# Where the second layer's expert outputs are summed: an internal array, or the output itself

## The chip, the cores and the metric

The kernel runs on one core of a Trainium2 chip. The core has a matrix engine (PE), a vector engine (DVE), a scalar engine (ACT), a general engine (POOL), and a queue engine (SP) that mostly issues transfers. Each engine runs its own list of instructions in order, and the lists are tied together by semaphores. Transfers are carried by 16 DMA engines that all queues share. The metric is the device time of one execution in microseconds (us); the median of three runs before the change is 1024.19 us (1023.56 to 1030.92).

## The reference

Two transformer layers run over `x` of 4 sequences x 512 tokens x 256 features. Each layer is a cross-attention followed by a mixture of experts in which every token goes to its two best experts out of eight. Only the end of the second layer matters here:

```
x = x + L1_xattn(layernorm(x), ctx)           # residual after the attention
logits = layernorm(x) @ Wg                    # 8 experts, the best two of each token
comb   = softmax(top 2) * alpha               # weight of each (token, expert)
for e in range(8):
    a = gelu(hdn_e @ fc1_w[e] + fc1_b[e])     # 256 -> 1024
    y = a @ fc2_w[e] + fc2_b[e]               # 1024 -> 256
    out += y * comb[:, e]
return x + out
```

The result of a token is thus its residual (with the biases `fc2_b`, weighted) plus two weighted expert rows. 2048 tokens times two choices are 4096 rows. With the inputs of the reference the experts of the second layer get 748, 469, 588, 538, 499, 487, 330 and 437 rows.

## The kernel before

**Routing.** For each of the four sequences `route_steps(L1, b)` computes the two experts of each token, and scatters the normalised rows (256 features, the token's number, the weight) into the internal array `rows`, one region for each expert (L851, an indirect DMA on POOL). Then it adds the weighted biases to the residual `x[b]` in SBUF (L888) and stores `x[b]` as 512 KB into the internal array `acc` (L889, on the SP queue). `acc` has 2048 rows for the tokens, and 128 spare rows behind them, which are filled with zeros at the very start of the kernel (L129, a DMA on POOL).

**The expert tiles.** `moe(L1, ...)` then walks over tiles of 128 rows. Each expert's rows are cut into tiles, and the last tile of an expert is usually not full. For 748, 469, ... 437 rows that makes 6 + 4 + 5 + 5 + 4 + 4 + 3 + 4 = 35 tiles, 4480 places for 4096 rows; the very last tile has 437 - 3 x 128 = 53 rows. The program has code for up to 39 tiles: 35 unconditionally, the rest under `tc.If`, which these inputs don't enter. For each tile,

- `load_rows` (L989, SP) fetches 128 rows; `load_w` (L973, SP) fetches the expert's two weight matrices where the expert changes;
- `turn` transposes the rows on PE and scales them (L1011, L1017), and computes in `to` (L1004, DVE) where each row of the result belongs: the token's number, or, for a place that holds no row, a spare row (`aside`, L947: 2048 plus the partition's number);
- `up` multiplies by the first matrix (L1031) and applies gelu (L1040, ACT); `down` multiplies by the second (L1052), weights the rows on DVE (`yw`, L1056), and adds them to `acc` by an indirect DMA with addition, issued on POOL (L1069).

Since the additions all go into one array, each of these indirect DMAs waits until the one before has landed. The order of PE's work is written out by hand, as is SP's in the expert parts. On the other engines, and for SP in the second attention, a planner at build time places the instructions.

**The end.** After the last tile `layer1_experts` copies the 2048 token rows of `acc` into the kernel's output `out` (L1163), a DRAM to DRAM transfer of 2.1 MB on the SP queue. It waits for all additions. Then the program ends: SP waits for the semaphores of all transfers, and the engines drain and meet (all at L1238).

**In the first layer** the same function stores its rows differently (L1059): a plain indirect DMA into `ys`, whose bounds check has `oob_is_err=False`. There `aside` is a row number behind the array's end, so that places without a row are not written at all.

Of the kernel before, what the change touches and what calls it, by code (L numbers as in the profile page):

```python
# [8 lines left out]
F32 = mybir.dt.float32  # L9
# [4 lines left out]
ALU = mybir.AluOpType  # L14
# [3 lines left out]
P = 128  # L18
NB = 4
S = 512  # L20
# [3 lines left out]
D = 256  # L24
# [31 lines left out]
def two_layers(ctx: ExitStack, tc: tile.TileContext, io, out):  # L56
    nc = tc.nc
# [11 lines left out]
    dram = ctx.enter_context(tc.tile_pool(name="dram", bufs=1, space=bass.MemoryType.DRAM))  # L69
# [4 lines left out]
    def t4(shape, name, dt=F32):  # L74
        return k4.tile(shape, dt, tag="k4", name=name)
# [4 lines left out]
    def tsmall(shape, tag, dt=F32):  # L80
        return sm.tile(shape, dt, tag=tag, name=tag, bufs=2 if tag[:3] in ("rt_", "tp_", "tt_") else None)
# [7 lines left out]
    def mm_ps(name):  # L89
        return ps_m.tile([P, 512], F32, tag="m", name=name)  # L90
# [30 lines left out]
    nc.gpsimd.tensor_copy(tile_f, tile_i)  # L121

    rows = dram.tile([EX * REGION, ROW], F32, tag="rows", name="rows")
    acc = dram.tile([NB * S + P, D], F32, tag="acc", name="acc")

    ys = dram.tile([2 * NB * S, D], F32, tag="ys", name="ys")
    zeros = t4([P, ROW], "zeros")
    nc.gpsimd.memset(zeros, 0.0)
    nc.gpsimd.dma_start(out=acc[NB * S :, :], in_=zeros[:, 0:D])  # L129
    def after(a, b, why):  # L130
        info = mybir.DependencyInfo(mybir.DependencyClass.Sync, mybir.DependencyReason.DATA)
        tc.add_manual_dep(a.ins, b.ins.name, info, reason=why)
# [10 lines left out]
    x = []  # L143
# [42 lines left out]
    for e in range(EX):  # L186
        i = nc.gpsimd.dma_start(
            out=rows[e * REGION : (e + 1) * REGION, :].rearrange("(p k) r -> p k r", p=P),
            in_=zeros.unsqueeze(1).to_broadcast([P, REGION // P, ROW]),
# [5 lines left out]
        out=ys[:, :].rearrange("(p k) d -> p k d", p=P),  # L195
        in_=zeros[:, 0:D].unsqueeze(1).to_broadcast([P, 2 * NB * S // P, D]),
# [497 lines left out]
    def top2(lg, ne, pick):  # L694

        shape = [P, NT, ne]
        by_e = desc[:, ET0 - ne :].unsqueeze(1).to_broadcast(shape)

        def over(v):
            return v.unsqueeze(2).to_broadcast(shape)  # L700

        m = []
        l = lg
        for k in range(2):
            mk = tsmall([P, NT], f"tp_m{k}")
            nc.vector.tensor_reduce(mk, l, AX.X, ALU.max)
            o = pick[:, k]
            nc.vector.tensor_tensor(o, l, over(mk), ALU.is_equal)
            nc.vector.tensor_tensor(o, o, by_e, ALU.mult)
            at = tsmall([P, NT], f"tp_at{k}")  # L710
            nc.vector.tensor_reduce(at, o, AX.X, ALU.max)
            nc.vector.tensor_tensor(o, o, over(at), ALU.is_equal)
            m.append(mk)
            if k == 0:
                l = tsmall(shape, "tp_l")
                nc.vector.scalar_tensor_tensor(l, o, TAKEN, lg, ALU.mult, ALU.add)
        d = tsmall([P, NT], "tp_d")
        nc.vector.tensor_tensor(d, m[1], m[0], ALU.subtract)
        e = tsmall([P, NT], "tp_e")
        nc.scalar.activation(e, d, AF.Exp)  # L720
        den = tsmall([P, NT], "tp_den")
        nc.vector.tensor_scalar(den, e, 1.0, None, ALU.add)
        w = tsmall([P, 2, NT], "tp_w")
        nc.vector.reciprocal(w[:, 0], den)
        nc.vector.tensor_tensor(w[:, 1], e, w[:, 0], ALU.mult)
        return w
# [53 lines left out]
    def route_steps(L, b):  # L780
# [22 lines left out]
        st = L.state.pop(b)  # L803
# [3 lines left out]
        w = top2(lg, ne, pick)  # L807
# [11 lines left out]
        r = const.tile([P, NT + 1, ne], F32, tag=f"run{L.n}{b}", name=f"run{L.n}_{b}")  # L819
# [4 lines left out]
        at = tsmall([P, NT, ne], "rt_atp")  # L824
# [23 lines left out]
        for k in range(2):  # L848
            for t in range(NT):

                i = nc.gpsimd.indirect_dma_start(  # L851
                    out=rows[:, :],
                    out_offset=bass.IndirectOffsetOnAxis(ap=pos_i[:, k, t : t + 1], axis=0),
                    in_=buf[:, k, t, :], in_offset=None,
                    bounds_check=EX * REGION - 1, oob_is_err=False,
# [25 lines left out]
        for k in range(0, NT, 2):  # L881
# [4 lines left out]
                )  # L886
            xs = x[b][:, k : k + 2, :]
            nc.vector.tensor_tensor(xs, op.rearrange("p (j d) -> p j d", d=D), xs, ALU.add)  # L888
        nc.sync.dma_start(out=acc[b * S : (b + 1) * S, :].rearrange("(t p) d -> p t d", p=P), in_=x[b])  # L889
        yield  # L890

    def tile_table(L):
# [59 lines left out]
    def ring_slots(L):  # L952

        slots = []
        if L.n == 0:
            for s in range(RING):
                if s % 2 == 0:
                    t = tbig(f"w0s_{s}").rearrange("p (h w) n -> p h (w n)", w=2)
                h = 2 * (s % 2)
                slots.append((t[:, h, :], t[:, h + 1, :]))  # L960
        else:
            for s in range(RING):
                w1 = res.tile([P, W1ROW], F32, tag=f"ctxT{s}", name=f"w1s_{s}")
                w2 = t8([P, FF1 // P * D], f"w2s_{s}")
                slots.append((w1, w2))
        for s in range(RING):
            for part in range(2):
                ring_load(L, slots[s], part, slice(0, 1))
        return slots
# [5 lines left out]
    def moe(L, slots, side=iter(())):  # L975
# [69 lines left out]
        def down(i):  # L1045
            w2 = slots[i % RING][1]
            aT = aTs.pop(i)
            rt = rts.pop(i)
            to = tos.pop(i)
            op = mm_ps(f"y{n}_{i}")[:, 0:D]  # L1050
            for f in range(nf):
                nc.tensor.matmul(  # L1052
                    op, aT[:, f, :], w2[:, f * D : f * D + D], start=(f == 0), stop=(f == nf - 1)
                )
            y = t4([P, D], f"yw{n}_{i}")
            nc.vector.tensor_scalar(y, op, rt[:, D + 1 : D + 2], None, ALU.mult)  # L1056
            where = bass.IndirectOffsetOnAxis(ap=to[:, 0:1], axis=0)
            if n == 0:
                st = nc.gpsimd.indirect_dma_start(  # L1059
                    out=ys[:, :], out_offset=where, in_=y, in_offset=None,  # L1060
                    bounds_check=2 * NB * S - 1, oob_is_err=False,
                )
                if y_stores:
                    tc.declare_no_dep(st.ins, group="ys", reason="no two tiles have the same row")
                    after(st, ys_fill, "the rows are filled before")
                tc.add_to_no_dep_group("ys", st.ins)
                y_stores.append(st)
            else:
                nc.gpsimd.indirect_dma_start(  # L1069
                    out=acc[:, :], out_offset=where, in_=y, in_offset=None,  # L1070
                    bounds_check=NB * S + P - 1, oob_is_err=True, compute_op=ALU.add,
                )

        def run(lo, hi, at=None):
            for i in range(lo, min(lo + 2, hi)):
                load_rows(i)
            for i in range(lo, min(lo + RING, hi)):
                for part in range(2):
                    load_w(i, part)
            turn(lo)  # L1080
            for i in range(lo, hi + 1):
                if i < hi:
                    if i + 2 < hi:
                        load_rows(i + 2)
                    up(i)
                    if i + RING < hi:
                        load_w(i + RING, 0)
                    if i + 1 < hi:
                        turn(i + 1)
                if i > lo:  # L1090
                    down(i - 1)
                    if i - 1 + RING < hi:
                        load_w(i - 1 + RING, 1)
                if i >= 8:
                    next(side, None)
                if i == at:
                    used.append(
                        nc.values_load(
                            total[0:1, 0:1], engines=None, min_val=0, max_val=TILES,
                            skip_runtime_bounds_check_because="at most TILES: one tile of each expert is not full",  # L1100
                        )
                    )
# [57 lines left out]

    def layer1_experts():
        moe(L1, ring_slots(L1))
        nc.sync.dma_start(  # L1163
            out=out.rearrange("b s d -> (b s) d").rearrange("(q r) d -> q (r d)", q=16),
            in_=acc[0 : NB * S, :].rearrange("(q r) d -> q (r d)", q=16),
        )

    with tc.manual_schedule(engines={mybir.EngineType.PE}):
        route = layer0_attention()
        with tc.manual_schedule(engines={mybir.EngineType.SP}):  # L1170
            sts = layer0_experts(route)
        layer1_attention(sts)
        with tc.manual_schedule(engines={mybir.EngineType.SP}):
            layer1_experts()
# [67 lines left out]
```

## Time and profile before

| Quantity | us |
|---|---|
| median of three runs | 1024.19 |
| the profiled execution, as timed | 1006.65 |
| its span, first to last instruction | 1004.9 |
| first matmul of a second-layer tile | 732.30 |
| last matmul of a tile ends (982.53 + 7.07) | 989.60 |
| last weighting on DVE ends (989.64 + 0.48) | 990.12 |
| last addition issued on POOL | 991.39 |
| copy `out<-acc` issued on SP | 995.22 |

The span of the profile is the time from the first instruction to the last on the core. The profiled execution's own time is 1.75 us above its span, and the median of the runs without a profile is 17.5 us above that. Times in the views are counted from the start of the span. A line of the chain of waits gives start, length and the work (engine, tile, source line); "POOLq" or "SPq" is an engine's instruction queue, with its waits and issue, rather than its arithmetic.

### The profile page before, as it was taken

Reading aid. Unit: us, or ns where it says so; the run is one execution under the profiler, and the core shown is the slowest. Engines: PE = TensorE matmul, PEld = TensorE weight load, DVE = VectorE, ACT = ScalarE, POOL = GpSimd, SP = SyncE. Lnnn points to the kernel's source line nnn. Section 1 sums busy time; section 2 is a strip of 40 time slices with the busy share of each in tenths; the row PEclk is TensorE's granted clock in tenths of the full one; section 3 lists DMA queues with packets and bytes.
Section 4 is the critical chain, followed back from the end, with each engine's and each line's share of the span. In section 5 each row is a group of like instructions: output and inputs, shape, how many; then the busy total and the mean of one; then the engine's idle time right before and its main releaser. Section 6 shows DMA issues by size and latency. Waiting matters only on the chain.

```text
span 1004.9 us, 15208 instructions
## 1 busy us (share of the span) xinstructions
PE 906.9 (90%) x5506; PEld 674.1 (67%) x5506; DVE 441.4 (44%) x1257; ACT 328.4 (33%) x727; POOL 225.5 (22%) x263
## 2 busy tenths in 40 slices
PE   5888989988989999889989989999489999999993
PEld 2445464635579997456656656657289999999993
DVE  6555473725623322854755666656511111111110
ACT  2222221220111111565754555554132323232230
POOL 3310103031502222000120330422601221121211
PEclk9899999998999999989999999999589999999997
DMA  8999802011149794500000101101816868678963
GB/s 319 283 255 237 267 1 92 24 57 44 57 156 293 245 313 163 174 1 2 22 1 2 64 22 43 64 1 38 299 33 183 256 203 259 179 252 240 326 191 100
DMA packets 55033, 144.65 MB, mean 144 GB/s; under 512 B 6454, under 2 KB 32877, under 8 KB 48776
## 3 DMA queue, kind: packets, MB, share of 16 engines
q1 hardware_dynamic: 39224, 104.98, 31.2%
q0 software_dynamic: 15440, 38.63, 15.2%
q8 instruction: 46, 0.75, 0.3%
q14 instruction: 35, 0.29, 0.1%
q10 hardware_dynamic: 288, 0.00, 0.0%
HBM read 142.02 MB, written 42.14 MB: 183 GB/s over the span
## 4 chain that ended last, share of the span: by engine, by line
PE 45%; issue 4%; ACT 4%; DVE 4%; DMA 2%; POOL 1%; SPq 0%; POOLq 0%; ACTq 0%; DVEq 0%
PE hp L1031 12%; PE y L1052 11%; PE s L578 6%; PE a2t L601 5%; PE o L626 4%; DVE p L587 2%; ACT p L591 2%; PE q L562 1%; DMA acc<-yw,to 1%; PE v L480 1%; PE k L466 1%; PE wo L641 1%; POOL rowbuf L769 1%; PE ht L1011 1%; ACT L591 1%
## 5 line engine op out<-in xcount | busy, mean ns | idle before, releaser
L1031 PEld LDWEIGHTS hp<-hT,w1s 128*128 128x128 f32 x1120 | 133.3, 195 | 3.6 <-DVE hT L1017 1.9
L1031 PE MATMUL hp<-hT,w1s 128*128 128x128 f32 x1120 | 133.8, 279 | 1.2 <-DVE hT L1017 1.2
L1040 ACT ACTIVATE aT<-hp,w1s 128x128 f32<-128x128 f32 x280 | 76.2, 384 | 168.4 <-issue 168.4
L1052 PE MATMUL y<-w2s,aT 128*128 128x256 f32 x560 | 126.5, 379 | 0.0
L1052 PEld LDWEIGHTS y<-w2s,aT 128*128 128x128 f32 x560 | 103.8, 190 | 12.7
L1069 POOL DMA_INDIRECT acc<-yw,to x35 | 54.0, 1541 | 212.1 <-DVE to L1004 137.1
L587 DVE CUSTOM_DVE_ANT_0 p<-s,mbias 128x1024 f32<-128x1024 f32 x64 | 75.8, 1220 | 57.5 <-PE s L578 57.5
L591 ACT ACTIVATE p<-p,s_nm 128x1024 f32<-128x1024 f32 x64 | 73.4, 1147 | 68.1 <-DVE s_nm L587 68.1
L1056 DVE TENSOR_SCALAR yw<-y,row 128x256 f32<-128x256 f32 x63 | 30.5, 484 | 136.5 <-PE y L1052 136.5
L601 PEld LDWEIGHTS a2t<-ident,p 128*128 128x128 f32 x512 | 57.1, 143 | 46.7 <-issue 25.3
L601 PE MATMUL a2t<-ident,p 128*128 128x128 f32 x512 | 72.7, 283 | 12.0 <-ACT a2T L606 5.6
L851 POOL DMA_INDIRECT rows<-rowbuf,rt_posi x64 | 64.0, 1000 | 57.3 <-DVE rt_posi L831 20.9
L578 PE MATMUL s<-kT,q2T 64*128 64x512 f32 x256 | 72.1, 669 | 2.1 <-DVE s_nm L587 2.1
L1017 DVE TENSOR_SCALAR hT<-ht,w1s 128x128 f32<-128x128 f32 x70 | 25.5, 406 | 94.7 <-PE ht L1011 90.9
L626 PE MATMUL o<-a2T,v 128*64 128x128 f32 x1024 | 63.3, 276 | 1.7 <-ACT kT L471 1.1
L626 PEld LDWEIGHTS o<-a2T,v 128*64 128x64 f32 x1024 | 55.4, 137 | 11.5 <-issue 7.5
L606 ACT COPY a2T<-a2t 128x512 f32<-128x512 f32 x96 | 53.6, 582 | 22.5 <-PE a2t L601 22.2
L292 PE MATMUL s<-ctxT,q0T 128*128 128x512 f32 x128 | 60.0, 614 | 0.5 <-DVE q0T L270 0.5
L322 PE MATMUL hq<-a0T,ctxn 128*128 128x512 f32 x128 | 59.7, 621 | 0.6 <-DVE a0T L256 0.6
L623 POOL COPY s_rs<-s_tot 128x128 f32<-128x128 f32 x32 | 11.5, 358 | 207.6 <-DVE s_tot L593 128.2
L1031 PEld LDWEIGHTS hp<-hT,w0s 128*128 128x128 f32 x448 | 54.3, 192 | 2.9 <-DVE hT L1013 1.5
L1031 PE MATMUL hp<-hT,w0s 128*128 128x128 f32 x448 | 54.7, 275 | 1.0 <-DVE hT L1013 1.0
(239 smaller groups left out, 1211.5 us busy)
## 6 DMA issues: line engine op xcount, KB each, us to landing
w1s<-in_w1p SPq DMA_DIRECT2D x38, 1030.0 KB
w2s<-in_w2p SPq DMA_DIRECT2D x38, 1024.0 KB
rows<-zeros POOLq DMA_DIRECT2D x8, 2064.0 KB, 58.5
w0s<-in_w1p SPq DMA_DIRECT2D x31, 512.0 KB
w0s<-in_w2p SPq DMA_DIRECT2D x31, 512.0 KB
row<-rows SPq DMA_DIRECT2D x63, 129.0 KB
ctxT<-in_ctxT SPq DMA_DIRECT2D x4, 1024.0 KB
ctxn<-in_ctx SPq DMA_DIRECT2D x4, 1024.0 KB
```

Of the source, the lines that this page charges most:

```text
L292: nc.tensor.matmul(sp[:, h, :], st["qT"][:, c, bass.ts(t, P)], ctxT[b][:, c, bass.ts(h, 512)], start=(c == 0), stop=(c == NC - 1),)
L322: nc.tensor.matmul(op, ctxn[b][:, j, bass.ts(c, P)], aT[:, j, :], start=(j == 0), stop=(j == NJ - 1))
L578: nc.tensor.matmul(sps[r][:, k, :], st["qT"][at, n, bass.ts(t, P)], st["kT"][at, n, bass.ts(k, 512)], start=True, stop=True,)
L587: nc.vector.tensor_tensor_reduce(p, sps[r].rearrange("p h n -> p (h n)"), st["mbias"][:, t, :], -ATT_SCALE, -ATT_SCALE * LEAST, ALU.add, A ...
L591: nc.scalar.activation(p, p, AF.Exp, bias=nm, scale=-1.0, accum_out=tot[:, r : r + 1])
L601: nc.tensor.transpose(pt[:, bass.ts(j, P)], p[:, bass.ts(4 * g + j, P)], ident)
L626: nc.tensor.matmul(op[r * HD : r * HD + HD, :], st["v"][:, j, bass.ts(2 * n + r, HD)], aT[:, r, bass.ts(j, P)], start=(j == 0), stop=(j == ...
L851: i = nc.gpsimd.indirect_dma_start(out=rows[:, :], out_offset=bass.IndirectOffsetOnAxis(ap=pos_i[:, k, t : t + 1], axis=0), in_=buf[:, k, ...
L1031: nc.tensor.matmul(o, w1[:, c * ff + f * P : c * ff + f * P + P], hT[:, c, :], start=(c == 0), stop=(c == NC - 1),)
L1040: nc.scalar.activation(aT[:, f, :], hp[:, f // 4, bass.ts(f % 4, P)], AF.Gelu_apprx_tanh, bias=w1[:, at : at + 1])
L1052: nc.tensor.matmul(op, aT[:, f, :], w2[:, f * D : f * D + D], start=(f == 0), stop=(f == nf - 1))
L1069: nc.gpsimd.indirect_dma_start(out=acc[:, :], out_offset=where, in_=y, in_offset=None, bounds_check=NB * S + P - 1, oob_is_err=True, compu ...
```

## The change

The internal array `acc` goes. The residual of a sequence is stored straight into `out`, and the indirect DMAs add their rows to `out` as well. The copy at the end goes. As `out` has no spare rows, the bounds check is now at 2047 and without an error: rows with a number of 2048 and more are to be left out. The kernel's planner orders accesses to its own arrays by itself; for `out` the order is now given by hand: the first addition after the four stores of the residual, every other addition after the one before.

```diff
-    acc = dram.tile([NB * S + P, D], F32, tag="acc", name="acc")
...
-    nc.gpsimd.dma_start(out=acc[NB * S :, :], in_=zeros[:, 0:D])
+    flat = out.rearrange("b s d -> (b s) d")
+    written = []
...
-        nc.sync.dma_start(out=acc[b * S : (b + 1) * S, :].rearrange("(t p) d -> p t d", p=P), in_=x[b])
+        written.append(
+            nc.sync.dma_start(out=flat[b * S : (b + 1) * S, :].rearrange("(t p) d -> p t d", p=P), in_=x[b])
+        )
...
-                nc.gpsimd.indirect_dma_start(
-                    out=acc[:, :], out_offset=where, in_=y, in_offset=None,
-                    bounds_check=NB * S + P - 1, oob_is_err=True, compute_op=ALU.add,
+                st = nc.gpsimd.indirect_dma_start(
+                    out=flat, out_offset=where, in_=y, in_offset=None,
+                    bounds_check=NB * S - 1, oob_is_err=False, compute_op=ALU.add,
                 )
+                for w in written:
+                    after(st, w, "one addition to a row at a time")
+                written[:] = [st]
...
         moe(L1, ring_slots(L1))
-        nc.sync.dma_start(
-            out=out.rearrange("b s d -> (b s) d").rearrange("(q r) d -> q (r d)", q=16),
-            in_=acc[0 : NB * S, :].rearrange("(q r) d -> q (r d)", q=16),
-        )
```

`after(a, b, why)` makes instruction `a` wait for `b`; where `b` is a transfer, for its landing.

## The prediction

> **What bounds the kernel now.** I read the page's busy times first, then the chain of waits over its last 45 us, then the waits of the SP queue, then the instructions of the program's end (source line L1238), and last the indirect DMAs of both layers. The page says that PE is the engine with the work:
>
> ```profile
> PE 906.9 (90%) x5506; PEld 674.1 (67%) x5506; DVE 441.4 (44%) x1257; ACT 328.4 (33%) x727; POOL 225.5 (22%) x263
> ```
>
> In the expert tiles of the second layer PE has no gap: a tile is 3.57 us (hp), 0.22 (ht) and 3.46 (y), 7.25 us together. POOL's additions run beside that. Only at the very end does the chain leave PE and go over to the additions:
>
> ```profile
> 964.63 3.57 PE hp L1031 x32
> 968.21 0.22 PE ht L1011 x2
> 968.42 3.47 PE y L1052 x16
> ...
> 986.95 3.69 DMA acc<-yw,to
> 990.64 0.03 issue
> 990.67 0.02 POOLq L1069
> 990.68 0.50 issue
> 991.18 0.31 POOLq L1098
> 991.49 1.44 POOL acc L1069
> ```
>
> The last addition but one lands at 990.64, and the last one starts on POOL at 991.39, though its rows were ready at 990.12. It waited for the landing, not for data. The chain stops there, because nothing on a computing engine follows. What follows is on the SP queue (waiting line and work, total, times, longest):
>
> ```profile
> SPq L1163 <- DMA acc<-yw,to: 22.0, 1, 22.0
> SPq L1238 <- DMA out<-acc: 7.4, 1, 7.4
> ```
>
> The copy waits for the last addition, is issued at 995.22, takes 0.62 us to issue, and the program's end then waits 7.4 us for it. The end itself (count: shortest/median/longest ns, first and last start):
>
> ```profile
> L1238 SPq EVENT_SEMAPHORE  x14: 17/28/28, 995.9 to 1004.8; - x14
> L1238 POOLq DRAIN  x3: 46/115/3538, 992.8 to 1004.6; - x3
> ```
>
> Cut into short windows, that view shows eight of SP's waits between 995.9 and 996.3, nothing until 1003.7, then four more; SP drains at 1004.0, the engines meet from 1004.1, and the span ends at 1004.9. So some 0.8 us pass between the start of the meeting and the end. The other line matters as much: POOL's drain starts at 992.8, behind the last addition, and takes 3.54 us, until 996.35. Today it is covered by the copy.
>
> **What the Trainium skill says.** "DMA: Bandwidth & Descriptors", section "Rules for kernel authors", says that an accumulating DMA must not overlap another access of the same bytes, and that one has to wait for the earlier DMA's semaphore. So the additions have to stay a chain in either version. The trace agrees: POOL waited six times, 34.7 us in all, for an addition to land. The same page, section "Anatomy of one DMA — SWDGE (gpsimd) path", fits a transfer as 2.0 us and bytes at 436 GB/s. It is fitted on another queue; for the 2.1 MB copy it gives an estimate of 2.0 + 4.8 = 6.8 us, and the trace shows 7.4, which I use. "Runtime: NRT & Kernel Launch", section "The ~15µs preamble/postamble breakdown", puts 9 to 15 us around a program. Here the median lies 19.3 us above the profiled span; the measurement decides, and I take this gap as unchanged, since nothing in it belongs to the edited lines.
>
> **The change part by part.**
>
> *The copy goes.* One issue of 0.62 us and one wait of 7.4 us leave the path. What is late next is POOL's drain: SP could meet the others at about 995.2 to 995.8 (its twelve waits take some 0.05 us each, and the last addition landed at about 995.1), but POOL is only there at 996.35. The meeting that began at 1004.1 begins there: 1004.1 - 996.35 = **7.75 us saved**. The drain was not on the path before, so its length without the copy is unknown. If POOL need not drain so long, the gain is up to 1.1 us more (995.2); if it takes even longer once nothing covers it, the gain shrinks, and I allow 0.5 us. I take it as it is.
>
> *The bounds check and the empty places.* The addition takes more POOL time than the plain store of the first layer, which already has the check without an error:
>
> ```profile
> L1059 POOL DMA_INDIRECT ys<-yw,to x28: 972/972/1170, 293.4 to 394.4; - x28
> L1069 POOL DMA_INDIRECT acc<-yw,to x35: 1532/1539/1588, 748.1 to 991.4; - x35
> ```
>
> The 0.57 us may be the addition's (they stay) or the check's (they go). In the tiles it does not matter, since PE's 7.25 us cover it. On the final chain stand two additions, so it is 0 to 0.57 for the first of them; I take 0. Then the last tile has 53 rows in place of 128; 75 are left out. Today each addition moves 144 packets, 128 rows and 16 others:
>
> ```profile
> q0 software_dynamic: 144, 0.13, 26.1%
> ```
>
> In the first layer the last two stores had 16 and 48 rows and landed 2.4 and 2.8 us after their issue, so 32 rows cost 0.4. The full additions at the end land in 3.7. The last one can come down to 2.8 if it behaves like the store with 48 rows, which is 0.9 less (its own share of the check included), or stay at 3.7 if an omitted row costs as much as a written one. I take **0.6**. Both together: 0 to 1.5 us.
>
> *The zero fill at the start* (128 KB; 0.78 us on POOL at 3.06). POOL next waits 5.4 us for a small load, so its time is hidden. Its bytes compete with the first load of `x`, which lands at 4.87 and is what DVE begins with: 128 KB at the page's 319 GB/s of that slice are 0.4 us at most, nothing at least. I take 0.1.
>
> *The four stores of the residual* have the same size, issuer and source; only the address changes, so nothing. They are issued at 580 to 723 and the first addition at 748, which is the cover: even a store that started 20 us later would be in time. The last one also has nothing urgent behind it: the six weight loads had been issued by 705, and the row loads wait for the scatters of `rows`.
>
> *The waits given by hand.* Each addition already waits for its predecessor, so one wait takes the place of another. Behind it on POOL stand only later additions; nobody but the end waits for them, apart from the buffers of `yw`. Price zero, as long as an addition lands within about 7.25 - 0.75 = 6.5 us of its issue on average (0.75 from a landing to the next start, 990.64 to 991.39). Today:
>
> ```profile
> DMA to landing us min/median/max: 3.6/5.0/7.9
> ```
>
> **Sum.** 7.75 + 0.6 + 0.1 = 8.45 us, so a profiled span of 996.4 from 1004.9, and **1015.7 us** as the median. The bounds of the terms (7.25 to 8.85, 0 to 1.5, 0 to 0.4) give 1013.4 to 1016.9.
>
> **The rivals.**
> *Over 1% faster.* POOL's drain shrinks along with the copy, and check, empty places and start all pay in full: 8.85 + 1.5 + 0.4 = 10.75, so 1013.4. Or the planner, which orders DVE, ACT and POOL anew at each build, does better around 696 to 713, where the eight copies of the last sequence's rows (7.28 us on POOL) stand behind eight scatters on the chain; four scatters fewer ahead of them, at 1.27 us each (719.49 to 720.76), would give 5 us more than the main case, and 1010.7. For it: the long drain is an oddity beside drains of 0.05 and 0.12. Against it: it needs nearly everything at once, or an order that nothing in the edit touches directly.
> *Slower.* Additions into `out` land later than those into `acc`. The point where this decides is 6.5 us on average. If all landed as the slow ones of today do (7.3 to 7.9 us after their issue; I take 7.6), the period would be 7.6 + 0.75 = 8.35 rather than 7.25: 35 x 1.1 = 38 us, less 8.45, so 1054. From 6.74 us on (8.45 / 35 above 6.5), the loss outweighs the saved copy. For it: six additions already wait for a landing, and `out` lies in another allocation. Against it: the copy wrote 2.1 MB into `out` in 7.4 us, near the rate of the estimate above, so `out` takes writes well; and the changed kernel moves fewer rows.
> *The copy goes and the end still waits*, for instance if the semaphores of the additions are awaited in another order: the drain bounds this, and it gives 7.25, 1016.9, the main case again.
>
> **How the numbers follow.** The main case has a chance of 0.50, the faster rival 0.36, the slower one 0.14. About 1%, 10 us, is what a measurement of this kernel can tell from no change, and the main case lies just inside that bound, so some of the faster rival's chance is scatter. The predicted time is that of the main case. Its own range is 1013.4 to 1016.9; the three runs of before spread over 7 us, and half of that on each side gives 1010 to 1020. The better order of the planner is in that, and 1 us more at the top is for an order that gets a little worse. What is left out is the slow landing, and a little of the faster case.
>
> **What would show it.** Right: no row for the copy, the last matmul of a tile still near 989.6, the last addition with about 69 packets (53 + 16), the end's meeting starting within 1.5 us of that addition's landing, and a span near 996.4. The addition's POOL time at 0.97 or 1.54 us tells whose the 0.57 us were. Wrong: tiles longer than 7.25 us on PE or POOL waiting for most additions (the slow rival), a drain that ends much before or after 996, or a first tile that doesn't start at 732 (the planner).

## The result, and the profile after

The changed kernel takes 1019.49 us in the median (1013.38 to 1022.41, 17 runs), the kernel before 1024.19 us (1021.26 to 1030.92, 17 runs). Run against run the ratio is 0.994, with a 95% interval of 0.992 to 0.996: 6.1 us less, between 4.1 and 8.2. That is inside the bound of 1%, and the whole interval lies on the faster side.

The profiled execution of the changed kernel, however, has a span of 1020.5 us, 15.6 us *more* than the one shown of before. A reader who compares the two pages would conclude that the change lost time. So the first thing to do is to cut both spans into the same stages: the second attention, the last routing, the expert tiles, and the end. The view gives, for each stretch, its length, the busy time and instructions of each engine, then the granted clock of PE, the share of the DMA engines and the rate. Before:

```profile
430.00:705.00 275.00, 258.55 (x2051) 172.52 (x2050) 168.26 (x457) 151.26 (x284) 59.20 (x88) 0.97 0.08 25
705.00:732.30 27.30, 9.84 (x27) 4.68 (x25) 14.85 (x71) 2.30 (x4) 16.06 (x17) 0.56 0.71 270
732.30:990.00 257.70, 256.80 (x1748) 241.74 (x1748) 47.52 (x137) 77.52 (x281) 52.41 (x34) 0.99 0.69 207
990.00:1004.90 14.90, 0.00 (x0) 0.00 (x0) 0.13 (x1) 0.00 (x0) 1.54 (x1) 0.64 0.47 150
```

After, cut at the same work to within a few instructions (the lengths of the routing and of the tiles are made equal by the cut):

```profile
435.00:728.00 293.00, 263.47 (x2045) 174.80 (x2042) 167.80 (x453) 148.68 (x279) 59.76 (x87) 0.93 0.07 24
728.00:755.30 27.30, 9.54 (x26) 4.50 (x24) 13.95 (x70) 2.65 (x4) 15.18 (x17) 0.56 0.71 269
755.30:1013.00 257.70, 256.59 (x1748) 241.34 (x1748) 47.68 (x138) 77.25 (x281) 52.37 (x34) 0.99 0.67 206
1013.00:1020.50 7.50, 0.00 (x0) 0.00 (x0) 0.17 (x1) 0.00 (x0) 1.54 (x1) 0.74 0.10 12
```

The second attention, which the change doesn't touch, took 18 us longer by these cuts, with practically the same number of instructions, and PE was idle for 13 of them (29.5 us against 16.5). The granted clock was 0.93 rather than 0.97, but that is not where the loss begins. When one PE instruction is compared with the same one of before, the changed kernel is 2.4 us behind from 433 to 569 us, then 12.5 us behind by 594, and 22.3 us behind by 687; between these two steps, from 594 to 647 us, the lag doesn't change. Both steps are pauses. Behind each stand transposes of the attention (`a2t`). The two pages, before and after, give the busy time of that group, the mean ns of one, then PE's idle time ahead of them and what ended most of it:

```profile
L601 PE MATMUL a2t<-ident,p 128*128 128x128 f32 x512 | 72.7, 283 | 12.0 <-ACT a2T L606 5.6
L603 PE MATMUL a2t<-ident,p 128*128 128x128 f32 x512 | 76.0, 291 | 23.2 <-ACT combT L881 14.9
```

PE waits for the copy `combT` on ACT for 7.7 and 7.2 us there, where it waited for 1.6 us at most before. The chain of waits puts 6.38 us of the first pause (from 569.74) and 3.65 and 2.52 us of the second (from 650.92 and 654.85) down to "another core or an unknown queue", so the profile does not say what was waited for. In the first pause PEclk is 1.00 until 572.9 us and 0.50 from then to 583, so the lower clock came in the pause, not ahead of it. The change is not the cause: the same two pauses stand in the profiles of experiments 1 to 4, with the internal array and without it, and are missing in those of experiments 5 to 8, again with both kernels.

The rest agrees. From the first matmul of the second-layer tiles to the last it is 257.3 us before and 257.1 after. The last row of the stages is the change: 14.9 us have become 7.5. Instruction by instruction, each engine's order is the same in both kernels, apart from the two transfers that are gone.

Because of that, I compare kernels from here on by a length that lies behind the pauses: the **tail**, from the end of the last matmul to the end of the span. It was 1004.9 - 989.6 = 15.3 us and is now 1020.5 - 1012.65 = 7.85 us. The end of the chain after (start, length, work):

```profile
1009.99 3.73 DMA out<-yw,to
1013.72 0.02 issue
1013.75 0.02 POOLq L1073
1013.76 0.82 issue
1014.59 0.31 POOLq L1105
1014.89 1.44 POOL out L1073
```

It is the same chain: the last addition but one lands, then the last one starts. What comes behind it is now this (the end of the program, cut at 1018 to 1019.6 us):

```profile
L1241 SPq EVENT_SEMAPHORE  x11: 28/28/28, 1018.4 to 1019.1; - x11
L1241 SPq DRAIN  x2: 7/10/13, 1019.1 to 1019.2; - x2
L1241 POOLq DRAIN  x1: 3479/3479/3479, 1016.2 to 1016.2; - x1
```

SP sees the last addition land just before 1018.4 and is through at 1019.2. POOL's drain runs from 1016.2 to 1019.7, and only then do the engines meet. So the drain, which the copy had covered, is what ends last. The additions themselves are as they were:

```profile
L1073 POOL DMA_INDIRECT out<-yw,to x35: 1531/1538/1587, 770.9 to 1014.8; - x35
```

and the last of them, with 53 rows, still moves 144 packets, of which 91 are under 512 B (the transfers from 1014.6 us to the end):

```profile
DMA packets 145, 0.06 MB, mean 11 GB/s; under 512 B 91, under 2 KB 144, under 8 KB 144
...
q0 software_dynamic: 144, 0.05, 9.2%
```

91 is 16 and 75: a row that is left out still costs a packet, only a tiny one (8 bytes in the trace, where a row that is written takes 1 KB).

### The profile page after: what moved, and what is told of

It reads as the page before. It is cut to its first block, busy times and chain, and to the rows that moved or that the text cites. A ratio compares the mean times of both kernels' runs of the same rounds, so it can differ in the third digit from the quotient of the medians.

```text
span 1020.5 us, 15204 instructions
## 1 busy us (share of the span) xinstructions
PE 920.9 (90%) x5506; PEld 679.6 (67%) x5506; DVE 439.4 (43%) x1257; ACT 328.3 (32%) x727; POOL 225.6 (22%) x262
## 4 chain that ended last, share of the span: by engine, by line
PE 46%; issue 4%; ACT 4%; DVE 3%; DMA 2%; another core or an unknown queue 1%; POOL 1%; SPq 0%; POOLq 0%; ACTq 0%; DVEq 0%
PE hp L1035 12%; PE y L1056 11%; PE s L580 7%; PE a2t L603 5%; PE o L628 4%; DVE p L589 2%; ACT p L593 2%; DMA out<-yw,to 1%; PE q L564 1%; PE k L468 1%; PE v L482 1%; PE wo L643 1%; PE ht L1015 1%; POOL rowbuf L771 1%
## 5 line engine op out<-in xcount | busy, mean ns | idle before, releaser
L1073 POOL DMA_INDIRECT out<-yw,to x35 | 53.9, 1540 | 212.5 <-DVE to L1008 124.9
L603 PEld LDWEIGHTS a2t<-ident,p 128*128 128x128 f32 x512 | 59.5, 148 | 60.5 <-issue 27.8
L603 PE MATMUL a2t<-ident,p 128*128 128x128 f32 x512 | 76.0, 291 | 23.2 <-ACT combT L881 14.9
L580 PE MATMUL s<-kT,q2T 64*128 64x512 f32 x256 | 79.2, 723 | 1.4 <-DVE s_nm L589 1.4
L294 PE MATMUL s<-ctxT,q0T 128*128 128x512 f32 x128 | 62.2, 633 | 0.5 <-DVE q0T L272 0.5
L324 PE MATMUL hq<-a0T,ctxn 128*128 128x512 f32 x128 | 61.9, 640 | 0.5 <-DVE a0T L258 0.5
```

Source lines behind the costliest of these rows:

```text
L294: nc.tensor.matmul(sp[:, h, :], st["qT"][:, c, bass.ts(t, P)], ctxT[b][:, c, bass.ts(h, 512)], start=(c == 0), stop=(c == NC - 1),)
L324: nc.tensor.matmul(op, ctxn[b][:, j, bass.ts(c, P)], aT[:, j, :], start=(j == 0), stop=(j == NJ - 1))
L580: nc.tensor.matmul(sps[r][:, k, :], st["qT"][at, n, bass.ts(t, P)], st["kT"][at, n, bass.ts(k, 512)], start=True, stop=True,)
L603: nc.tensor.transpose(pt[:, bass.ts(j, P)], p[:, bass.ts(4 * g + j, P)], ident)
L1073: st = nc.gpsimd.indirect_dma_start(out=flat, out_offset=where, in_=y, in_offset=None, bounds_check=NB * S - 1, oob_is_err=False, compute_ ...
```

## The experiments

**1. The copy alone** (`no_copy`):

```diff
         moe(L1, ring_slots(L1))
-        nc.sync.dma_start(out=out..., in_=acc[0 : NB * S, :]...)
```

> The kernel before without the copy at the end; additions still go into the internal array, so out is never written. Measured as the tail: from the end of the last matmul to the end of the span, 15.3 us before, 7.9 us after the change. Theory (the whole gain is the copy): the tail is 7.8 to 8.2 us, the last addition takes 1.54 us on POOL and lands about 3.7 us after its issue, and POOL's drain of about 3.5 us ends last. In time 7.4 us less than before, a ratio of 0.993. Rival (adding into out, or the omitted rows, gives part of the gain): the tail stays at 9 us or more. The zero fill at the start is kept: if it costs the 0.2 us by which the changed kernel starts earlier, the first work on DVE is at 4.87 us as before, and not at 4.67.

The ratio to the kernel before is 0.992 (0.9894 to 0.9946), with medians of 1014.26 us against 1024.35. The last matmul ends at 1005.29 (998.22 + 7.07), the span at 1012.8: a tail of 7.5 us. The copy is thus all of the gain, and adding into `out` gives nothing that the internal array, without the copy, would not have given. First work on DVE is at 4.98 us; more on that in experiment 6.

**2. The new bounds check alone** (`skip_rows`):

```diff
-                    bounds_check=NB * S + P - 1, oob_is_err=True, compute_op=ALU.add,
+                    bounds_check=NB * S - 1, oob_is_err=False, compute_op=ALU.add,
```

> The kernel before with the new bounds check (2047, no error) on the internal array; copy and all else kept. As predicted: the last addition, with 53 rows of 128, lands some 0.6 us earlier, so the tail is 14.7 us rather than 15.3. Rival (an omitted row still costs a packet, as the changed kernel's 144 packets suggest): it lands 0.1 to 0.2 us earlier, the tail is 15.1 us, and the packets of the last addition stay 144. On POOL an addition takes 1.54 us if the addition itself is what costs, 0.97 if the error flag was.

```profile
1007.78 1.54 POOL L1069 DMA_INDIRECT acc<-yw,to  x1 [5.49 <-DVE yw L1056]
1010.48 0.48 DVE L1056 TENSOR_SCALAR yw<-y,row 128x256 f32<-128x256 f32 x1 [2.97 <-PE y L1052]
1012.18 1.54 POOL L1069 DMA_INDIRECT acc<-yw,to  x1 [2.86 <-DMA acc<-yw,to]
1015.98 0.62 SPq L1163 DMA_DIRECT2D out<-acc  x1
```

This is the end of its timeline. The copy, which waits for the last addition, is issued 3.80 us after that addition started (1012.18 to 1015.98); in the kernel before it was 3.83 (991.39 to 995.22). So 75 omitted rows out of 128 save nothing that can be seen, less even than the rival's 0.1 to 0.2 us. The repeats of experiment 7 agree: there the view gives the last landing itself, 3.6 us after its issue, with 128 rows written (before) and with 53 (after). The packets are 144, 91 of them small, as after the change; the tail is 15.4 us (1025.8 - 1010.43). And 1.54 us on POOL is the addition's own price, whichever the check.

**3. A small copy** (`small_copy`):

```diff
-            out=out...rearrange("(q r) d -> q (r d)", q=16), in_=acc[0 : NB * S, :]...
+            out=out...[0:P, :].rearrange("(q r) d -> q (r d)", q=16), in_=acc[0:P, :]...
```

> The kernel before with a copy of only the first 128 of 2048 rows, 131 KB in place of 2.1 MB; the other rows of out are not written. Theory (a fixed part and a part by bytes): 5 of the 7.4 us go, the tail is about 10.2 us. Rival 1 (the wait is a fixed price of any transfer at the end): the tail stays near 15.3. Rival 2 (it is all bytes): near 8.4.

The tail is 9.3 us (1014.6 - 1005.32), between the theory's 10.2 and the 8.4 of bytes alone. The SP queue's waits at the end:

```profile
SPq L1163 <- DMA acc<-yw,to: 21.8, 1, 21.8
SPq L1238 <- DMA out<-acc: 1.3, 1, 1.3
```

The wait for the copy falls from 7.4 to 1.3 us. So 6.1 of the 7.4 us went by bytes (1.97 MB fewer, so 322 GB/s, slower than the 436 GB/s of the fit that I took from the Trainium skill's "DMA: Bandwidth & Descriptors", section "Anatomy of one DMA — SWDGE (gpsimd) path", where it is made on another queue). A copy of only 128 rows still leaves the tail 1.8 us longer than none (9.3 against 7.5). Part of what it costs passes under POOL's drain, which lasts until 1012.0 while the copy is issued at 1010.95.

**4. Each addition twice, with half the weight** (`twice`), to see when the additions stop being free:

```diff
+                nc.vector.tensor_scalar(y, op, rt[:, D + 1 : D + 2], 0.5, ALU.mult, ALU.mult)
...
+                for _ in range(2):
                     st = nc.gpsimd.indirect_dma_start(out=flat, ..., compute_op=ALU.add)
                     for w in written: after(st, w, ...)
                     written[:] = [st]
```

> The changed kernel with each addition made twice with half the weight, so two chained indirect DMAs for a tile. Theory (the additions are hidden behind PE's 7.25 us per tile only as long as landing and restart stay below it): two of them take 8.6 us (3.8 + 0.5 each, few weight loads beside them) to 11.6 us (5.3 + 0.5 each), so the kernel is 45 to 150 us slower, and PE waits for buffers in the second layer's tiles. Rival (POOL is not on the path whatever it does): at most 5 us slower, from one more landing at the end.

1154.22 us in one run, 130 us above the kernel before (1024.35), and 136 above an estimate of 1017.7 us for the changed kernel there (a ratio of 0.9935, the middle of its two measurements). The 70 additions start between 767.2 and 1143.5 us, so one takes 376.3 / 69 = 5.45 us and a tile 10.9, against PE's 7.25: 35 x 3.65 = 128 us. The waits in the tiles (who waited for whom, total, times, longest) show how it gets back to PE:

```profile
DVE yw L1063 <- DMA out<-yw,to: 227.5, 22, 17.1
POOL out L1077 <- DMA out<-yw,to: 139.3, 39, 8.0
...
PE hp L1035 <- DVE hT L1021: 78.4, 19, 10.0
```

The weighting on DVE waits for a landed addition, to have a free buffer; behind it in DVE's order stands the next tile's `hT`; and for that PE waits. The chain of additions was free only because it was shorter than PE's tile.

**5. What POOL's drain waits for** (`pool_waits`): a tiny memset on POOL that waits for the last addition's landing.

```diff
         moe(L1, ring_slots(L1))
+        i = nc.gpsimd.memset(const.tile([P, 1], F32, tag="last", name="last"), 0.0)
+        after(i, adds[GROUPS[1][0] - 1], "POOL waits for the last addition itself")
```

> The changed kernel with one tiny memset on POOL behind the landing of the last addition, so that POOL's drain at the end starts only then. Theory (the 3.5 us drain waits for the transfer that is still in flight): the drain shrinks to 0.1 to 1.3 us and the tail stays within 7.4 to 8.2 us. Rival (the drain is a fixed 3.5 us behind any indirect DMA): it starts at 5.8 us after the last matmul and the tail grows to about 10.1 us.

```profile
L1245 POOLq DRAIN  x3: 46/115/2872, 995.5 to 998.9; - x3
```

The memset runs at 995.50, so the last addition has landed by then; the drain behind it still takes 2.87 us, and the tail is 9.5 us (999.2 - 989.69). This is one run, and near the rival: most of the drain is not a wait for the transfer in flight. What POOL does in it, no view shows.

**6. The zero fill put back** (`zero_kept`). In the changed kernel the last addition starts 2.14 us after the last matmul, while in the kernels with the internal array it was 1.75 to 1.81 (five profiles); the chain showed 0.82 us of issue where there had been 0.50.

```diff
+    unread = dram.tile([P, D], F32, tag="unread", name="unread")
+    nc.gpsimd.dma_start(out=unread[:, :], in_=zeros[:, 0:D])
     flat = out.rearrange("b s d -> (b s) d")
```

> The changed kernel with the zero fill of 128 KB at the start put back, into an array that nobody reads. It asks where the 0.3 us come from by which the last addition starts later than in the kernels with the internal array (2.1 us after the last matmul rather than 1.8; issue of 0.82 rather than 0.50 us). Theory (the place of POOL's instructions in its stream: the missing transfer at the start shifts the rest): with the fill back it is 1.8 us and 0.50 again, and the tail 7.5 us. Rival (it comes with additions into out, or with the order given by hand): it stays at 2.1 us and 0.82, and the tail at 7.8. If the fill costs the start something, the first work on DVE is not before 4.9 us.

```profile
988.95 3.73 DMA out<-yw,to
...
992.71 0.52 issue
993.23 0.31 POOLq L1107
993.54 1.44 POOL out L1075
```

1.84 us and 0.52, and a tail of 7.5 us (999.1 - 991.60). So the missing instruction at the start costs the last addition 0.3 us, 990 us later; neither `out` nor the order by hand does. (With the fill put back this is one profile. Without it, experiments 5 and 7 show 2.10 and 2.06 us as well.) That it acts through the place of the later instructions in POOL's stream is my reading; no view shows the mechanism. As for the start: with the fill, the first work on DVE was at 4.71, 4.87, 4.98, 5.00, 5.12 and 5.12 us over six profiles, without it at 4.63, 4.67, 4.92, 4.92 and 4.94 over five (experiment 7 and the one after included). The averages differ by 0.15 us, less than either spreads, so the start's share is not shown.

**7. Both kernels again, on another chip** (`before_again`, `after_again`; no edit).

> The kernel before, unchanged, against itself. Theory (the profiled 1004.9 us of before was one execution with a high clock, and the median of 1024 is the usual one): ratio 1.000 within 0.003, profiled span near 1022, tail 15.3 us whatever the span. Rival (the 17.5 us lie outside the span, around the program): the span is again near 1005 and the time near 1024.

> The changed kernel again, beside the kernel before on the same chip. Theory (nothing changed but the tail and the 0.2 us at the start): 7.6 us less, a ratio of 0.9926, tail 7.9 us, first work on DVE at 4.67 us. Rival (something of the gain is given back in the body): a ratio of 0.995 or more with the same tail.

Before against itself: 0.9987 (0.9967 to 1.0008). The changed kernel: 0.9929 (0.9902 to 0.9955), 999.53 us against 1005.68. The tails are 14.9 and 7.8 us. The interval holds the 7.6 us that were expected and reaches down to 4.5, so a small loss in the body can't be ruled out by times; the stages above show none.

On the 17.5 us both expectations were wrong. The profiled span was short again, 997.7 us, but the times were short with it: 1005.65 us in the median, and 999.51 us for the profiled execution. Every execution on record with both numbers is 1.7 to 1.9 us above its span. So the 17.5 us do not lie around the program; they lie between one execution and another. The traces show most of such a difference. The two pauses stand in the profiles with spans of 1012.8, 1014.6, 1020.5 and 1025.8 us, and put PE 17 to 20 us behind in the second attention; the profiles without them have 993.5 to 1005.9 us. The profile shown of before is one without, and at 1006.65 us it was faster than any of the 17 runs of its kernel beside the changed one (1021.26 at the least). That those runs had the pauses fits the numbers, but no trace of them is kept.

Neither the chip nor the granted clock settles it. The chip on which the kernel before had a median of 1024.35 us, with 1017.14 at the least, took 1003.15 us for it in the one run beside experiment 6. And at the same granted clock of 0.956 the kernel before had spans of 1001.3, 1004.9 and 1015.3 us. What brings the pauses is open.

**8. The last addition but one earlier** (`early_down`): PE's order of the last two tiles changed.

```diff
+                    early = n == 1 and lo == 0 and i == hi - 1
+                    if early:
+                        down(i - 1)
                     up(i)
...
-                if i > lo:
+                if i > lo and not (i < hi and early):
                     down(i - 1)
```

> The changed kernel with PE's order of the last two tiles changed: the second matmuls of the last tile but one stand ahead of the first matmuls of the last one, so that the last addition but one starts 3.6 us earlier. Theory (the last addition waits for the landing before it): the last addition starts 0.9 to 1.2 us after the last matmul rather than 2.1, PE stalls 0.3 to 0.6 us for the gelu, the tail is 6.7 to 7.0 us, and from the first tile to the end it takes 0.3 to 0.9 us less than the changed kernel's 265 us; in time nothing that can be told from no change. Rival (something else on POOL delays it): the last addition starts 2 us after the last matmul as before, and the kernel loses the stall.

```profile
980.92 1.54 POOL L1073 DMA_INDIRECT out<-yw,to  x1 [2.87 <-DMA out<-yw,to]
983.24 3.72 PE L1056 MATMUL y<-w2s,aT 128*128 128x256 f32 x16 [0.51 <-ACT aT L1044]
987.00 0.48 DVE L1060 TENSOR_SCALAR yw<-y,row 128x256 f32<-128x256 f32 x1 [7.31 <-PE y L1056]
987.76 1.54 POOL L1073 DMA_INDIRECT out<-yw,to  x1 [5.31 <-DVEq L1119]
```

The last addition starts 0.80 us after the last matmul (986.96), so it did wait for the landing before it, as the theory said. The stall before that matmul group is 0.51 us, and the tail is 6.5 us; start and tail are a little below what was expected. From the first tile to the end, the length that was expected to shrink by 0.3 to 0.9 us, it takes 264.9 us, the changed kernel 265.0. From the second tile to the end (its first matmul at 735.94 here, 762.51 after the change, 739.68 before) it takes 257.6 us, the changed kernel 258.0, the kernel before 265.2. So the shorter tail is mostly handed back ahead of the last matmul, 0.51 us of it as the stall, and what remains, 0.0 to 0.4 us by where one starts to count, is not shown to be a gain. The ratio to before is 0.9905 (0.9882 to 0.9929): faster than before, and not to be told from the changed kernel's 0.9929.

## Why the prediction was right, and where it was not

The direction, the class and the main mechanism hold; the size was taken somewhat too large, 8.45 us against 7.4 in the tail and 6.1 (4.1 to 8.2) in time. The measured 1019.49 us lies in the stated range because that was widened for scatter: the sum of the terms alone allowed 1013.4 to 1016.9. In the terms of the prediction the tail closes to 0.1 us: 7.8 for the copy, nothing for the omitted rows, and 0.3 lost at the end to the missing zero fill.

- **"The copy goes", 7.75 us: right.** Experiment 1 alone gives 15.3 - 7.5 = 7.8. What was to be late next is late next: POOL's drain, 3.48 us as against 3.54, ends 0.5 us after SP is through. The two open ends (a drain that shrinks with the copy or grows without it) did not come true. The prediction had no reason for a drain of the same length, so that part of the hit is luck. Experiment 5 adds that the drain hardly depends on the last addition's transfer. The order of SP's waits mattered little.
- **"I take 0.6" for the omitted rows: wrong, it is 0.** This is the step that failed. It took the landings of the first layer's last two stores, 2.4 and 2.8 us, as those of 16 and 48 rows, and so as the price of a row. The rows were misread. The traffic of the store that started at 392.74 and landed after 2.4 us is 0.13 MB, all 128 rows; only the one of 394.40, which took 2.8 us, has 48 rows (0.05 MB). So even these stores don't show that fewer rows land earlier, and among additions 53 rows land as late as 128 (experiment 2). The packet count, which I quoted for before, shows after the change that the places are still there: 144, not the 69 that were to be the sign. Why an addition lands 3.7 us after its start and a plain store 2.4 to 2.8 is explained only for the 0.57 us on POOL; that the store moves four rows in a packet (32 packets of 4 KB) and the addition one (128 of 1 KB) may bear on the rest, and no run tests it.
- **0 of the 0.57 us for the check: right.** 1.54 us remain with either check.
- **The zero fill, 0.1 us: not shown.** 0.2 us in the pair of profiles, but the start scatters by 0.5. What I did not think of is that removing an instruction at the start could cost 0.3 us at the end (experiment 6).
- **The four stores and the hand-written waits, 0: right.** The tiles took 257.3 and 257.1 us. The bound that I gave for the additions, 6.5 us to land on average, was not reached: in the repeat of the changed kernel (experiment 7), where the view has landings, the median is 4.1 us. Experiment 4 puts the price of crossing it at 130 us. The slower rival was thus a real cliff, and the change does not go over it: `out` takes additions as `acc` did.
- **The gap of 19.3 us between the span and the median "taken as unchanged": unchanged, but misread.** I put beside it the 9 to 15 us that the Trainium skill's "Runtime: NRT & Kernel Launch", section "The ~15µs preamble/postamble breakdown", gives for the time around a program. No run here shows these: a time is 1.7 to 1.9 us above its span, and the rest is the difference between a profile without the two pauses and slower executions. The subtraction was harmless here only because what goes away lies behind the pauses.
- **The faster rivals** needed the drain to shrink or the planner to move things. Neither happened: each engine's order is unchanged. The sign that was named for the planner, a first tile that doesn't start at 732 us, did come (755.6), and with it a last matmul and a span far from the forecast; the two pauses made it, not the planner.

## What to carry to other kernels

A transfer at the end of a program costs its wait minus what would have ended just behind it: look for the second-latest thing at the end, here a drain of 3.5 us, before the whole wait is booked as a gain. Where two profiles differ in a stage that the change doesn't touch, line up the same instructions to find the place of the difference, and measure the change from one event to another inside its own stage; 7.4 us stood there clearly while the spans said plus 15.6. And a chained, accumulating transfer on a side engine is free until its period passes that of the engine it hides behind; then every tile pays the difference.

## What the runs showed of the hardware that was not expected

- A row that the bounds check of an indirect DMA leaves out still takes a packet (144 with 128 rows or with 53), of 8 bytes instead of 1 KB, and here saves no time (3.80 against 3.83 us).
- POOL's drain behind an indirect DMA takes 3.4 to 3.6 us at the end of the program, and still 2.87 us when the DMA has already landed.
- An indirect DMA with addition takes 1.54 us on POOL with either bounds check; the plain store of the same tile size in the first layer takes 0.97. The addition moves its 128 rows as 128 packets of 1 KB, the store as 32 of 4 KB.
- The removal of one transfer near 3 us moved an issue gap on POOL from 0.50 to 0.82 us near the end of the program, and putting one back undid it.
- The same kernel had medians of 1024 us in one set of runs and 1006 in another, at granted clocks that overlap (0.943 to 0.956, and 0.949 to 0.962). Two pauses of PE, of 5.7 to 7.7 us each, in the second attention, whose cause no view shows, are in the profiles of some executions and not of others.
